# Reciprocal roots of the layernorms: Newton steps on VectorE, or a power on GpSimd

## The chip, the cores and the metric

The kernel runs on one core of a Trainium2 chip. Time is that of one launch on the device, in microseconds (us). The core's engines work side by side, each through a queue of its own in strict order: TensorE (PE in the profile; its weight loads are PEld), VectorE (DVE), ScalarE (ACT), GpSimd (POOL) and SyncE (SP, which issues most transfers). An instruction waits on semaphores until the work of other engines that it needs has ended, and while it waits nothing behind it on the same engine starts.

## The reference

Input x is 2048 rows of 256 float32, with a context of 1601 rows of 256. Four sublayers follow each other; each normalises the rows of x first:

```
x = x + xattn0(layernorm(x), ctx)   # attention, then a second layernorm with gamma and beta
x = x + ffn0(layernorm(x))          # two shared experts and the best two of eight routed ones
x = x + xattn1(layernorm(x), ctx)   # attention in both directions, mixed by a gate
x = x + ffn1(layernorm(x))          # softmax over 8 gates, experts above 0.3, output matrix
layernorm(x) = (x - mean(x)) / sqrt(var(x) + 1e-5)
```

Mean and variance are taken over the 256 values of a row, so each row needs one reciprocal root. The layernorm inside xattn0 works on the same shape.

## The kernel before

Rows lie on 128 partitions, so x is 16 tiles of 128 rows, which stay in the on-chip memory for the whole kernel. A block is four tiles. A layernorm of n tiles runs `bn_stats` and `bn_aggr` for each tile (L179, L180, VectorE), which leaves n means and n variances per partition, and then `rstd_of` (L155) for the n reciprocal roots at once. That is 13 VectorE instructions on 128 x n values: add epsilon (L159), shift the bits right and subtract them from a constant (L161, L162) for a first guess, multiply the variance by -0.5 (L163), and three Newton steps of three instructions (L167, L168, L170). There are 23 such calls: 14 with n = 4, one with n = 8, eight with n = 2.

The order of every engine's queue is made when the program is built: a scheduler places each instruction by its own estimate of durations, so a change of one instruction's engine can move others. The stages, and where the calls lie in them:

- First attention (0 to 150 us and the rest of its last block to 197 us), four blocks of 512 queries. Scores of a block (L268) go to PSUM, ScalarE copies them (L270), VectorE keeps the running maximum (L276). The maxima are transposed (L293, L298, L301), VectorE subtracts them (L308), ScalarE takes the exponent (L311), PE multiplies by the values (L510), ScalarE copies the result (`oT`, L512), and the output projection (L401) reads it. GpSimd adds the 13 score tiles of a block up for the softmax's denominators (L442, L444), a chain of 12 instructions that starts with the next block's first maximum, and adds beta to x (L367). PE reads the sums at L518. The second layernorm (`after`, L393) and the first layernorm of the next sublayer (`settled`, L488, from which L187 makes -mean times root, and ScalarE the scaled rows at L192) are made for one block while the next is under way.
- Shared and routed experts (175 to 578 us). No reciprocal root lies there after 194 us.
- Second attention, first direction (578 to 825 us): the layernorms of four blocks (L948) at 599 to 623 us.
- Second attention, other direction (825 to 1098 us), with the gate and the last sublayer in pairs of tiles that are woven between the attention's matmuls. Here the eight calls with n = 2 lie. For each pair: transposes of the attention's rows (L219, `ob`), gate matmuls (L1105), `z` (L1109, L1110), update of x (L1111, L1113), `bn_stats`, the root, the normalised rows `h` (L201), transposes of `h` (L219), a copy (`hT_g`, L1133), the gates' and experts' matmuls (L1139), a softmax over eight (L1145 to L1159), the sum (L1166) and the store. The attention's value matmuls (L323) fill PE between these steps; the last pair has none left. GpSimd's queue holds indirect transfers there (`near_rows`, L1052) that gather rows of the other direction's result, four for each pair; `sg` (L1063, L1064) mixes them, and its buffers are reused, so later gathers wait for earlier mixes.

Of the kernel before, what the change touches and what calls it, by code (L numbers as in the profile page):

```python
# [9 lines left out]
F32 = mybir.dt.float32  # L10
I32 = mybir.dt.int32
U32 = mybir.dt.uint32
AF = mybir.ActivationFunctionType
ALU = mybir.AluOpType
# [3 lines left out]
P = 128  # L18
# [4 lines left out]
NT = S // P  # L23
# [16 lines left out]
EPS = 1e-5  # L40
# [4 lines left out]
def xattn_ffn_kernel(ctx: ExitStack, tc: tile.TileContext, t: dict, out: bass.AP):  # L45
    nc = tc.nc

    def sbuf(stack, name, bufs=1, side="left"):
        return stack.enter_context(tc.tile_pool(name=name, bufs=bufs, side=side, reuse_waits="tile"))


    const = sbuf(ctx, "const")
# [91 lines left out]

    make_identity(nc, ident)
    nc.gpsimd.memset(ones, 1.0)


    def copy(i, dst, src):
# [4 lines left out]

    def rstd_of(pool, mv, n, wide=BT):  # L155


        ve = pool.tile([P, wide], F32, name="ve")[:, :n]
        nc.vector.tensor_scalar(ve, mv[:, :n, 1], EPS, None, ALU.add)  # L159
        seed = pool.tile([P, wide], I32, name="seed")[:, :n]  # L160
        nc.vector.tensor_scalar(seed, ve.bitcast(I32), 1, None, ALU.logical_shift_right)  # L161
        nc.vector.tensor_scalar(seed, seed, -1.0, float(0x5F3759DF), ALU.mult, ALU.add)  # L162
        nc.vector.tensor_scalar(ve, ve, -0.5, None, ALU.mult)  # L163
        y = seed.bitcast(F32)
        for k in range(3):
            u = pool.tile([P, wide], F32, name="newton")[:, :n]
            nc.vector.tensor_tensor(u, y, y, ALU.mult)  # L167
            nc.vector.tensor_tensor(u, u, ve, ALU.mult)  # L168
            new = pool.tile([P, wide], F32, name=f"rstd{k}")[:, :n]
            nc.vector.scalar_tensor_tensor(new, u, 1.5, y, ALU.add, ALU.mult)  # L170
            y = new
        return y

    def stats_of(first, n, pool, wide=BT):

        st = pool.tile([P, wide, 6], F32, name="st")
        mv = pool.tile([P, wide, 2], F32, name="mv")
        for j in range(n):
            nc.vector.bn_stats(st[:, j, :], xs[:, first + j, :])  # L179
            nc.vector.bn_aggr(mv[:, j, :], st[:, j, :])  # L180
        return mv, rstd_of(pool, mv, n, wide)
# [147 lines left out]
    with ExitStack() as ph:  # L329
# [63 lines left out]
        def after(b, oT, rden, past):  # L393

            st = sp.tile([P, BT, 6], F32, name="st2")
            mv = sp.tile([P, BT, 2], F32, name="mv2")
            for j0 in range(0, BT, 2):
                ps = bank(ps_m)
                for k in range(2):
                    j = j0 + k  # L400
                    nc.tensor.matmul(  # L401
                        ps[:, k * D : (k + 1) * D], oT[:, j * P : (j + 1) * P], wofc, start=True, stop=True
                    )
                for k in range(2):
                    y = past[:, j0 + k, :]
                    nc.vector.scalar_tensor_tensor(
                        y, ps[:, k * D : (k + 1) * D], rden[:, j0 + k : j0 + k + 1], y, ALU.mult, ALU.add
                    )
                    nc.vector.bn_stats(st[:, j0 + k, :], y)
                    nc.vector.bn_aggr(mv[:, j0 + k, :], st[:, j0 + k, :])  # L410
            rs = rstd_of(sp, mv, BT)
            for j in range(BT):
                y, xt = past[:, j, :], xs[:, b * BT + j, :]
                nc.vector.scalar_tensor_tensor(y, y, mv[:, j, 0:1], gamma, ALU.subtract, ALU.mult)
                nc.vector.scalar_tensor_tensor(xt, y, rs[:, j : j + 1], xt, ALU.mult, ALU.add)
# [33 lines left out]
        for b in range(NB + 1):  # L449
            new = between = None  # L450
            if b + 1 < NB:
                h = rows_before(b + 1, fresh(b + 1))
            if b < NB:
# [27 lines left out]
                new = (b, e, acc, past)  # L481
# [19 lines left out]
            else:  # L501
                n, e, acc, past = last
# [357 lines left out]
    with ExitStack() as ph:  # L860
# [117 lines left out]
        for n_blk, blk in enumerate(blocks + [None]):  # L978
            new = between = None
            if blk is not None:  # L980
# [15 lines left out]
                new = (lo, w, e, acc)  # L996
# [18 lines left out]
    with ExitStack() as ph:  # L1015
# [176 lines left out]
        for b in range(NB + 1):  # L1192
            new = between = None
# [3 lines left out]
            if b < NB:  # L1197
# [3 lines left out]
                new = (b, e)  # L1201
# [3 lines left out]
            else:  # L1205
                n, e = last
# [82 lines left out]
```

## Time and profile before

| | us |
|---|---|
| median of three runs (lowest, highest) | 1098.29 (1097.05, 1099.68) |
| profiled execution, own time | 1099.73 |
| its span | 1097.9 |
| PE busy in it | 1052.9 |
| VectorE, ScalarE, GpSimd busy | 504.2, 342.6, 230.3 |

The profiled execution is 1.44 us above the median. Its mean granted TensorE clock is 0.976 of full speed. A line of a timeline gives the start, the duration, engine, line of the program, operation, the tile written and the tiles read, their shapes, and how many instructions were merged; in brackets stands the idle time of that engine just before it, and what ended it.

### The profile page before, as it was taken

To read this page: it belongs to the slowest core of one execution; us is meant where nothing else is said; L and a number is where in the kernel's file an instruction comes from. 1 tells how busy PE (TensorE), PEld (TensorE's weight loads), DVE (VectorE), ACT (ScalarE), POOL (GpSimd) and SP (SyncE) were. 2 spreads that over 40 slices of the span, in tenths; PEclk is the share of its full clock that TensorE was granted. 3 is DMA by queue.
4 is the path that set the end of the run, shared out by engine and by line. 5 is a ranking of instruction groups with operands and counts; after the bars stand their busy time and mean duration, and the time that the engine had idled before them with its cause. 6 is when DMAs were issued, how large, how long until landed. Compare 5 with 4: busy or idle time off the path is not lost. (4 is left out here: it accounts for less than half of the span.)

```text
span 1097.9 us, 11034 instructions
## 1 busy us (share of the span) xinstructions
PE 1052.9 (96%) x3718; PEld 654.4 (60%) x3718; DVE 504.2 (46%) x1271; ACT 342.6 (31%) x569; POOL 230.3 (21%) x236
## 2 busy tenths in 40 slices
PE   7999989999999999999999999999998979999994
PEld 5545548656556666666665644464763466675873
DVE  4777884422222222222223745442413766566764
ACT  3754634311111112112213435321403633333311
POOL 2066440032320011111111006603134312000000
PEclk9999988899999999999999999999999989999997
DMA  9070000911121411111104000010004212000000
GB/s 315 24 188 1 0 1 17 409 73 39 44 54 30 123 44 44 49 44 48 44 24 138 27 0 1 0 39 30 10 19 139 84 38 80 11 10 10 1 20 19
DMA packets 42326, 62.81 MB, mean 57 GB/s; under 512 B 10461, under 2 KB 30045, under 8 KB 42270
## 3 DMA queue, kind: packets, MB, share of 16 engines
q1 hardware_dynamic: 35342, 43.73, 12.4%
q0 software_dynamic: 5824, 17.32, 5.0%
q10 hardware_dynamic: 1104, 1.05, 0.3%
q8 instruction: 31, 0.51, 0.2%
q14 instruction: 25, 0.20, 0.1%
HBM read 42.65 MB, written 19.44 MB: 57 GB/s over the span
## 5 line engine op out<-in xcount | busy, mean ns | idle before, releaser
L794 PE MATMUL sc<-rew,rT 128*128 x288 | 129.6, 593 | 0.6 <-DVE rT L785 0.6
L706 PE MATMUL sc<-hT_f,ew 128*128 128x512 f32 x256 | 115.8, 608 | 0.0
L323 PE MATMUL mm<-vs,e 128*128 128x257 f32 (+1 forms) x416 | 97.8, 386 | 0.0
L268 PE MATMUL sc<-hT,ks 128*128 128x512 f32 (+1 forms) x208 | 91.6, 593 | 3.3 <-DVE m L279 3.3
L308 DVE TENSOR_TENSOR e<-e,tp 128x2048 f32<-128x2048 f32 (+3 forms) x48 | 86.7, 1860 | 12.7 <-PE tp L301 12.7
L311 ACT ACTIVATE e<-e 128x2048 f32<-128x2048 f32 (+3 forms) x48 | 74.3, 1571 | 51.3 <-DVE e L308 50.3
L268 PE MATMUL sc<-qs,hT 128*128 128x512 f32 (+2 forms) x256 | 88.1, 501 | 0.9 <-ACT hT L949 0.9
L1008 PE MATMUL mm<-e,hr 128*128 128x512 f32 (+2 forms) x256 | 88.0, 500 | 0.0
L323 PEld LDWEIGHTS mm<-vs,e 128*128 128x128 f32 (+1 forms) x416 | 79.1, 194 | 13.8 <-issue 2.8
L794 PEld LDWEIGHTS sc<-rew,rT 128*128 128x128 f32 x288 | 54.5, 190 | 54.2 <-issue 52.5
L270 ACT COPY e<-sc 128x512 f32<-128x512 f32 (+3 forms) x116 | 61.0, 534 | 81.7 <-PE sc L268 81.6
L276 DVE TENSOR_TENSOR m<-sc,m 128x512 f32<-128x512 f32 (+3 forms) x100 | 62.7, 627 | 51.8 <-ACT e L270 48.7
L706 PEld LDWEIGHTS sc<-hT_f,ew 128*128 128x128 f32 x256 | 49.6, 196 | 56.9 <-issue 55.8
L800 DVE TENSOR_TENSOR ract<-rsl,sc 128x512 f32<-128x512 f32 x36 | 24.8, 688 | 111.5 <-PE sc L794 108.0
L819 POOL DMA_INDIRECT rows_out<-rout,goes_to x36 | 35.0, 973 | 175.0 <-DVE rout L818 170.6
L268 PEld LDWEIGHTS sc<-qs,hT 128*128 128x128 f32 x256 | 48.0, 190 | 37.1 <-issue 26.8
L1008 PEld LDWEIGHTS mm<-e,hr 128*128 128x128 f32 x256 | 48.2, 190 | 35.3 <-issue 28.2
L268 PEld LDWEIGHTS sc<-hT,ks 128*128 128x128 f32 (+1 forms) x208 | 38.2, 186 | 50.1 <-issue 43.2
L814 PE MATMUL mm<-rew,raT 128*128 x288 | 68.0, 380 | 0.0
L711 ACT ACTIVATE sl<-sc 128x512 f32<-128x512 f32 x32 | 19.1, 597 | 132.4 <-PE sc L706 132.4
L798 ACT ACTIVATE rsl<-sc 128x512 f32<-128x512 f32 x36 | 21.5, 597 | 123.0 <-PE sc L794 123.0
L993 POOL TENSOR_TENSOR acc<-acc,e 128x512 f32<-128x512 f32 (+2 forms) x56 | 57.9, 1033 | 4.4
(267 smaller groups left out, 1459.7 us busy)
## 6 DMA issues: line engine op xcount, KB each, us to landing
rew<-in_ew_dram SPq DMA_DIRECT2D x24, 512.0 KB, 10.2
rows_in<-zero SPq DMA_DIRECT2D x1, 5011.5 KB, 21.5
rin<-rows_in SPq DMA_DIRECT2D x36, 128.0 KB, 2.1
g<-rows_out SPq DMA_DIRECT2D x8, 512.0 KB, 5.6
ew<-in_ew_dram SPq DMA_DIRECT2D x7, 512.0 KB, 5.4
rows_sub<-sgrow SPq DMA_DIRECT2D x12, 256.0 KB, 2.0
ctxT<-in_ctxT_dram SPq DMA_DIRECT2D x4, 512.0 KB, 6.2
out_dram<-xs SPq DMA_DIRECT2D x8, 256.0 KB, 2.1
```

Source lines behind the costliest of these rows:

```text
L268: nc.tensor.matmul(ps, kT[:, d, k * P : k * P + r], q[:, d, :], start=(d == 0), stop=(d == nd - 1))
L270: seen = [nc.scalar.copy(e[:r, k, :w], ps)]
L276: seen.append(nc.vector.tensor_tensor(m[:r, :w], ps, upto, ALU.max))
L308: nc.vector.tensor_tensor(part, part, bc[:r, :w].unsqueeze(1).to_broadcast([r, k1 - k0, w]), ALU.add)
L311: nc.scalar.activation(part, part, AF.Exp)
L323: nc.tensor.matmul(ov[:c, : D + 1], e[:r, k, j * P : j * P + c], v[:r, k, :], start=(k == 0), stop=(k == len(rows) - 1))
L706: nc.tensor.matmul(p, w[:, c, cols], hT[:, c, b * BW : (b + 1) * BW], start=(c == 0), stop=(c == DC - 1),)
L794: nc.tensor.matmul(p, rT[:, c, :], w[:, bass.ds(base + c * HID, HID)], start=(c == 0), stop=(c == DC - 1))
L814: nc.tensor.matmul(y, aT[:, hc, :], routed[2][:, bass.ds(base + hc * D, D)], start=(hc == 0), stop=(hc == NHC - 1))
L819: nc.gpsimd.indirect_dma_start(out=rows_out, out_offset=bass.IndirectOffsetOnAxis(ap=goes_to[:, s : s + 1], axis=0), in_=r, in_offset=None ...
L993: nc.gpsimd.tensor_tensor(acc[:, :w], acc[:, :w], e[:, k, :w], ALU.add)
L1008: nc.tensor.matmul(ov, hr[:, k, d * P : (d + 1) * P], e[:, k, :w], start=(k == 0), stop=(k == NT - 1))
```

## The change

`rstd_of` now takes two GpSimd instructions: the addition of epsilon, and a power, element by element, whose exponents are a tile that holds -0.5 everywhere. That tile is made once. All 13 VectorE instructions of each call go. In the changed file the new lines are L148, L160 and L162.

```diff
     make_identity(nc, ident)
     nc.gpsimd.memset(ones, 1.0)
+    power = const.tile([P, NT], F32, name="power")
+    nc.gpsimd.memset(power, -0.5)
...
         ve = pool.tile([P, wide], F32, name="ve")[:, :n]
-        nc.vector.tensor_scalar(ve, mv[:, :n, 1], EPS, None, ALU.add)
-        seed = pool.tile([P, wide], I32, name="seed")[:, :n]
-        nc.vector.tensor_scalar(seed, ve.bitcast(I32), 1, None, ALU.logical_shift_right)
-        nc.vector.tensor_scalar(seed, seed, -1.0, float(0x5F3759DF), ALU.mult, ALU.add)
-        nc.vector.tensor_scalar(ve, ve, -0.5, None, ALU.mult)
-        y = seed.bitcast(F32)
-        for k in range(3):
-            u = pool.tile([P, wide], F32, name="newton")[:, :n]
-            nc.vector.tensor_tensor(u, y, y, ALU.mult)
-            nc.vector.tensor_tensor(u, u, ve, ALU.mult)
-            new = pool.tile([P, wide], F32, name=f"rstd{k}")[:, :n]
-            nc.vector.scalar_tensor_tensor(new, u, 1.5, y, ALU.add, ALU.mult)
-            y = new
-        return y
+        nc.gpsimd.tensor_scalar(ve, mv[:, :n, 1], EPS, None, ALU.add)
+        rs = pool.tile([P, wide], F32, name="rstd")[:, :n]
+        nc.gpsimd.tensor_tensor(rs, ve, power[:, :n], ALU.pow)
+        return rs
```

## The prediction

> **What bounds the kernel now.** First the page: busy shares, then PE over 40 slices.
>
> ```profile
> PE 1052.9 (96%) x3718; PEld 654.4 (60%) x3718; DVE 504.2 (46%) x1271; ACT 342.6 (31%) x569; POOL 230.3 (21%) x236
> ...
> PE   7999989999999999999999999999998979999994
> ```
>
> PE is full but for the first slice, the last one and a few nines missing between. So a VectorE instruction saved is worth nothing by itself; a reciprocal root counts only where PE stands still for it, and PE's whole idle time is 45 us. Next, the timelines of PE, VectorE and GpSimd around the roots. The last root of all, and PE beside it and before it:
>
> ```profile
> 1081.74 0.17 DVE L159 TENSOR_SCALAR ve<-mv 128x2 f32<-128x2 f32 x1
> ...
> 1084.11 0.73 DVE L201 TENSOR_SCALAR h<-xs,mv,rstd 128x256 f32<-128x256 f32 x2
> ...
> 1066.17 0.78 PE L219 MATMUL tp<-ident,h 128*128 128x128 f32 x4 [0.80 <-DVE h L201]
> ...
> 1074.58 0.55 PE L219 MATMUL tp<-ident,ob 128*128 128x128 f32 x3 [1.28 <-DVE ob L1077]
> ...
> 1084.67 1.13 PE L219 MATMUL tp<-ident,h 128*128 128x128 f32 x4 [6.87 <-DVE h L201]
> ```
>
> A root takes 1084.11 - 1081.74 = 2.37 us, and only the last pair has PE idle for all of it. For the seven pairs before, value matmuls cover the root but for 0.25, 0.45, 0.41, 0, 0.20, 0.82 and 0.80 us (PE's idle time at L219 `h`). Now the first pair, with GpSimd's queue:
>
> ```profile
> 902.81 1.41 POOL L1052 DMA_INDIRECT near_rows<-rows_sub,near  x1 [22.30 <-ACT z L1110]
> ...
> 905.70 0.16 DVE L159 TENSOR_SCALAR ve<-mv 128x2 f32<-128x2 f32 x1
> ...
> 908.07 0.73 DVE L201 TENSOR_SCALAR h<-xs,mv,rstd 128x256 f32<-128x256 f32 x2
> ```
>
> Its root is made while GpSimd issues four gathers, until 908.2. Last, the first attention, where GpSimd's chains of sums lie beside roots:
>
> ```profile
> 93.27 14.77 POOL L444 TENSOR_TENSOR acc<-acc,e 128x512 f32<-128x512 f32 x11
> ...
> 102.03 0.62 DVE L159 TENSOR_SCALAR ve<-mv 128x4 f32<-128x4 f32 x1
> ...
> 105.47 2.29 DVE L308 TENSOR_TENSOR e<-e,tp 128x2048 f32<-128x2048 f32 x1
> ...
> 112.78 3.67 PE L401 MATMUL mm<-wofc,oT 128*128 128x256 f32 x8 [2.71 <-ACT oT L512]
> ...
> 149.44 3.78 PE L401 MATMUL mm<-wofc,oT 128*128 128x256 f32 x8 [3.34 <-ACT oT L512]
> ```
>
> PE waits at L401 for `oT`, which waits on ScalarE for L308's results.
>
> **Price of the new root.** From the variances to the first use: VectorE to GpSimd 0.15 us (an L276 ends at 124.68, L442 starts at 124.83), the addition 0.20, GpSimd's wait on itself 0.07 (sums of 1.27 us follow each other every 1.34), the power p, GpSimd to its reader 0.06 (sums end at 73.66, L518 starts at 73.72): 0.48 + p. No row shows a power. GpSimd's groups that bound it:
>
> ```profile
> L367 POOL TENSOR_TENSOR xs<-xs,beta 128x1024 f32<-128x1024 f32 x4 | 9.4, 2360 | 64.9 <-ACT past L192 49.4 <-DVE newton L167 15.5
> ...
> L993 POOL TENSOR_TENSOR acc<-acc,e 128x256 f32<-128x256 f32 x14 | 10.2, 725 | 1.1
> ...
> L683 POOL COPY h_f<-place_i 128x16 int32<-128x16 int32 x2 | 0.4, 206 | 2.2 <-DMA rows_in<-h_f,slot 2.2
> ...
> L617 POOL CAST e<-e8i 128x8 f32<-128x8 int32 x1 | 0.2, 181 | 0.0
> ```
>
> So p is at least 0.18 (nothing with data is cheaper at this size) and, as its upper end, 2.36, the dearest arithmetic row. With two to eight values per partition it is nearest to the 0.2 us rows; I take 0.40, twice the copy, for the many steps of a power. The root then costs 0.88 us instead of 2.37 (a gain of 1.49) wherever GpSimd is free. Each 0.1 us on p is 0.1 us on every root.
>
> The Trainium skill's GPSIMD Engine Reference (section "Performance versus the Vector engine") speaks against the change: elementwise work stays on VectorE, about 2x faster. The trace agrees for large tiles (1270 ns for 128x512 on GpSimd, 627 ns on VectorE at L276). By that rule two instructions of 0.16 us would be 0.64 instead of my 0.60, so the sum would be 0.4 us higher. The same page (section "Instruction dispatch") puts a first call of a freshly loaded routine at about 6 us; no row here shows that; it would let the first root end at about 14.5 instead of 10.6, and PE wants that block at 17.25, so the sum would stay.
>
> **What else moves.** The order in which the built program queues its work is changed too; these are the places that touch PE.
>
> 1. Cover is taken away. Between the gate matmuls (L1105) and the transposes of `h`, the changed kernel has fewer value matmuls (0.43 us each): 13 for 18 (first pair), 14 for 19 (third), 6 for 11 (fourth), 11 for 16 (sixth and seventh); for the second, six of 12 and two more scores (0.86). That is about 2.15 us, near the scheduler's own gain, and the work is done later. So the 1.49 us are not PE's gain: PE comes 2.15 us earlier and the root 1.49.
> 2. GpSimd's queue has the first root behind the four gathers, and the second behind the next four.
> 3. In the first attention, VectorE's L187 now waits for GpSimd's sums and stands ahead of L308, where Newton steps stood and ran.
>
> **The sum, last stage**, with 0.88 us a root. From `z` to the variances, waits counted from L1105's end, 0.56 from L201's start to PE (as at 908.07 and 908.63), 0.24 for the modelled tail of the cover:
>
> - First pair. `z` started at 900.59; the gathers end 7.6 us later, the root 0.73 after that, PE can transpose at 8.9; its cover ends at 5.6. The wait of 3.2 is partly given back, since ScalarE's copy waits for a gather's landing at 909.6 in either case: L1139 starts at 10.5 for 10.26, with four value matmuls fewer done: +0.24 + 1.72 = +2.0.
> - Second: same queue; transposes at 8.9 for 9.1 but 0.9 us less cover: wait about 1.5 at L219 and L1139 for 0.7: +0.8.
> - Third: `z` to variances 5.45 (two softer steps now come before, L1098 after), 0.2 + 5.45 + 0.88 + 0.56 - 6.26 = 0.8 for 0.41: +0.4. Fourth: 6.95 + 0.88 + 0.56 - 7.98 = 0.4 for 0: +0.4. Fifth: as the third, 0.8 for 0.20: +0.6.
> - Sixth: 0.2 + 3.83 + 0.88 + 0.56 - 4.97 = 0.5 for 0.82: -0.3. Seventh: 0.2 + 3.9 + 0.88 + 0.56 - 4.97 = 0.57 for 0.80: -0.2 (VectorE is free for `z` earlier there, since value matmuls or transposes now precede L1105).
> - Those moved matmuls lie ahead of the last `ob`: 11 for 4, so its 1.28 us wait goes: -1.3. Last pair: no cover, -1.5.
>
> Sum: +0.9.
>
> **The sum, first attention.** The built order starts block 1's sums some 3 us earlier (54.3, their maximum waits no longer for scaled rows), so PE's wait at 73.72 falls by 1.2. In block 2 the sums then end near 104.9, and L187 lets L308 start at 105.8 where it did at 105.47; the lead is lost. In block 3, two L510 are now ahead of the scores, the sums end near 142.5 (before, 140.9), the root at 143.2, and L308 starts 0.9 after 142.43; PE's L401 comes at 150.7 for 149.44: +1.3. No value is given to the roots at 184 to 194: PE has expert matmuls there, and GpSimd is idle. Those at 599 to 623 cost nothing either way: PE reaches the first rows at 617.83, they were ready at 605.6. If that cover were gone, it would be the root's 0.88. The transfers on SyncE keep their order; GpSimd's scatters at 221 start earlier, and PE works on shared experts until past 340.
>
> Together +2.2 us. The profiled execution's 1099.73 would become 1101.9; against the median of 1098.29, 1.44 lower, that is 1100.5. Ten roots lie on PE's path (eight in the last stage, two in the first), so p moves this by 10 us per us: 1098.3 at p = 0.18, 1120 at 2.36.
>
> **The rivals.**
>
> - A dear power. If it takes 1 us or more (2.36: 1120), all gates wait, and VectorE stands still behind L187, L415 and L201. For it: no row of a power, and Newton needs 13 steps. Against: 8 values at most. From p = 0.4 it is slower by over 0.2%. Price at p = 1.2: 1108.5.
> - The other side: PE's holes close. If the moved matmuls fill what PE now waits for, in the pairs 1 to 7 (0.25 + 0.45 + 0.41 + 0.20 + 0.82 + 0.80 = 2.9, and the 1.28), with the last pair's 1.5, the time is 1098.3 - 5.7 = 1092.6. For it: the same amount of value matmuls is left for later places. Against: two roots behind eight gathers. It decides if the root stays within the scheduler's own figure, which the removed cover puts at 2.37 - 2.15 = 0.22 to 0.65, that is p below 0.2, and the gathers start 3 us earlier.
> - No effect: 1098.3, if the queues' losses and the last pair's gain cancel.
>
> **How the numbers follow.** Forecast with p from 0.2 to 0.7 and 3 us for the reordering: 0.50; dear power 0.23; holes closed 0.20; no effect 0.07. A change within 0.2% (2.2 us) is about what a measurement here cannot tell from none. The forecast lies at that bound: slower 0.27, same 0.19, faster 0.04 of its 0.50. Dear power is all slower, closed holes all faster, no effect 0.06 same and 0.01 faster. Together slower 0.50, same 0.25, faster 0.25. The range leaves out the dearer half of the dear powers and the ends of closed holes: 1093.5 to 1115; the forecast's own is 1097 to 1104.
>
> **What would show it.** VectorE 299 instructions fewer (972) and near 450 us busy; GpSimd 47 more. First L162 of n = 2: its start-to-start spacing gives p. GpSimd's first pair: power right behind the fourth gather; PE's idle at that L219 near 3 us; the last L219 idle 5.4 for 6.87; `ob`'s 1.28 gone; PE's L401 waits 4 us twice. Wrong if p is over 1 us, if the gathers start earlier, or if the early stage keeps its lead of 1.2 us.

## The result, and the profile after

The changed kernel takes 1107.62 us (median of six runs, 1104.40 to 1110.78) where the kernel before takes 1098.42 beside it: ratio 1.0086, 95% interval 1.006 to 1.0112. It is slower, by about 9 us. The forecast was 1100.5, its own range 1097 to 1104, its range over all rivals 1093.5 to 1115. The direction and the wide range hold; the likeliest case was 7 us too fast. The profiled execution of the changed kernel took 1110.78 us (span 1108.7, granted clock 0.971), the slowest of the six, 3.2 above the median: differences between the two traces are to be read with that in mind.

First the page: busy times, then PE over 40 slices. All lines after `rstd_of` stand nine lower than before (L201 is now L192, L219 is L210, L401 is L392, L1139 is L1130).

```profile
PE 1056.0 (95%) x3718; PEld 657.0 (59%) x3718; DVE 457.1 (41%) x972; ACT 342.7 (31%) x569; POOL 258.7 (23%) x283
...
PE   8998989999999999999999999999999879999995
```

VectorE has lost 299 instructions and 47.1 us of work. PE stands still for 52.7 us of its span, where it was 45.0, and its 3718 matmuls take 1056.0 us, where they took 1052.9. Next, GpSimd's groups for the new instruction, by shape (count, then busy time and the mean of one in ns):

```profile
L162 POOL TENSOR_TENSOR rstd<-ve,power 128x4 f32<-128x4 f32 x14 | 14.5, 1037 | 1.2
L162 POOL TENSOR_TENSOR rstd<-ve,power 128x2 f32<-128x2 f32 x8 | 5.7, 712 | 0.7
L162 POOL TENSOR_TENSOR rstd<-ve,power 128x8 f32<-128x8 f32 x1 | 1.7, 1655 | 0.1
```

The power p that the forecast put at 0.40 us takes 0.71 for two values per partition, 1.04 for four, 1.66 for eight: 0.39 us and 0.16 more for every value. Next, the last stage: GpSimd around the first gate root, and PE around the first, second, seventh and last (in brackets PE's idle time just before, and what ended it).

```profile
905.62 1.41 POOL L1043 DMA_INDIRECT near_rows<-rows_sub,near  x1 [21.88 <-ACT z L1101]
...
909.95 1.01 POOL L1043 DMA_INDIRECT near_rows<-rows_sub,near  x1 [0.30 <-issue]
910.99 0.25 POOL L160 TENSOR_SCALAR ve<-mv 128x2 f32<-128x2 f32 x1
911.32 0.72 POOL L162 TENSOR_TENSOR rstd<-ve,power 128x2 f32<-128x2 f32 x1
...
912.64 0.45 PE L210 MATMUL tp<-ident,h 128*128 128x128 f32 x1 [3.64 <-DVE h L192]
...
916.10 4.86 PE L1130 MATMUL sc<-ewg,hT_g 128*128 128x264 f32 x16
...
938.08 0.78 PE L210 MATMUL tp<-ident,h 128*128 128x128 f32 x4 [2.32 <-DVE h L192]
...
940.15 4.78 PE L1130 MATMUL sc<-ewg,hT_g 128*128 128x264 f32 x16
...
1075.73 0.78 PE L210 MATMUL tp<-ident,h 128*128 128x128 f32 x4 [0.81 <-DVE h L192]
...
1086.58 0.55 PE L210 MATMUL tp<-ident,ob 128*128 128x128 f32 x3 [0.67 <-DVE ob L1068]
...
1095.45 1.13 PE L210 MATMUL tp<-ident,h 128*128 128x128 f32 x4 [5.60 <-DVE h L192]
```

The root is made right behind the fourth gather, as foreseen, and PE waits 3.64 us for it (foreseen 3.2). The last wait has fallen from 6.87 to 5.60. New are the lines at 916.10 and 940.15: the same 16 matmuls took 3.77 and 3.74 us before. Last, the first attention, GpSimd, VectorE and PE together:

```profile
42.61 1.66 POOL L162 TENSOR_TENSOR rstd<-ve,power 128x8 f32<-128x8 f32 x1
...
51.78 1.12 PE L259 MATMUL sc<-qT,kT 128*128 128x512 f32 x2 [0.96 <-ACT past L381]
...
81.22 0.88 DVE L406 SCALAR_TENSOR_TENSOR xs<-past,rstd,xs 128x256 f32<-128x256 f32 x2 [1.25 <-POOL rstd L162]
...
104.73 0.23 POOL L160 TENSOR_SCALAR ve<-mv 128x4 f32<-128x4 f32 x1
105.04 1.03 POOL L162 TENSOR_TENSOR rstd<-ve,power 128x4 f32<-128x4 f32 x1
106.10 0.16 DVE L178 SCALAR_TENSOR_TENSOR nmean<-mv,rstd 128x4 f32<-128x4 f32 x1 [7.22 <-POOL rstd L162]
...
113.19 3.54 PE L392 MATMUL mm<-wofc,oT 128*128 128x256 f32 x8 [5.89 <-ACT oT L503]
...
151.34 3.78 PE L392 MATMUL mm<-wofc,oT 128*128 128x256 f32 x8 [4.96 <-ACT oT L503]
```

L178 is the L187 of the forecast: it waits for a root that stands behind GpSimd's chain of sums, and VectorE's L299 (once L308) starts behind it. PE's two waits were 2.71 and 3.34.

To place a loss, the traces are compared at three points that every kernel has: PE's first transposes of an expert's rows (366.56 before), the first transposes of the maxima in the last stage (885.10 before), and the last transposes of `h` (1084.67 before). The table gives the first arrival, then the two stretches, all from the timelines of PE in one profiled execution each, and the measured ratio.

| kernel | to the experts | to the last stage | last stage | ratio to before (95% interval) |
|---|---|---|---|---|
| before | 366.56 | 518.54 | 199.57 | 1 |
| changed | 370.96 | 517.17 | 207.32 | 1.0086 (1.006, 1.0112) |
| x1 multiplication, more expert work | 362.02 | | 198.91 | 1.011 (1.009, 1.013) |
| x2 gathers behind two roots | 371.50 | 517.45 | 202.40 | 1.0038 (1.0023, 1.0054) |
| x3 power for the gates only | 367.10 | 521.03 | 204.51 | 1.0054 (1.0035, 1.0073) |
| x4 power for the early roots only | 369.64 | 517.41 | 200.74 | 1.0018 (1.0003, 1.0033) |
| x5 multiplication, same work | 362.88 | 517.36 | 198.92 | 0.9942 (0.9922, 0.9962) |
| x6 power done twice | 377.19 | 517.32 | 212.03 | 1.0208 (1.0174, 1.0243) |
| x7 both places mended | 362.49 | 517.15 | 201.11 | 0.9981 (0.9957, 1.0005) |
| x8 power for the last root only | 367.04 | 521.40 | 199.31 | 0.9984 (0.9964, 1.0005) |
| x9 two early roots by Newton | 368.34 | 517.51 | 203.15 | 1.0017 (0.9997, 1.0038) |
| x10 power where GpSimd is free | 363.12 | 517.36 | 198.31 | 0.9956 (0.9942, 0.997) |
| x11 x10, last wait filled | 364.12 | 517.23 | 200.55 | 0.9939 (0.9919, 0.9958) |
| x12 x10 with two Newton steps | 365.39 | 517.46 | 196.75 | 0.9938 (0.9918, 0.9957) |

In the traces of before and after, the change loses 4.4 us ahead of the experts and 7.75 in the last stage, and gains 1.4 between them. PE's idle time grows by 3.2 us in the first stretch and by 5.65 in the last; the rest, 1.2 and 2.1, is matmuls that take longer.

### The profile page after: what moved, and what is told of

Same layout as the page of the kernel before. It is cut to its first block, busy times and chain, and to the rows that moved or that the text cites. A ratio compares the mean times of both kernels' runs of the same rounds, so it can differ in the third digit from the quotient of the medians.

```text
span 1108.7 us, 10794 instructions
## 1 busy us (share of the span) xinstructions
PE 1056.0 (95%) x3718; PEld 657.0 (59%) x3718; DVE 457.1 (41%) x972; ACT 342.7 (31%) x569; POOL 258.7 (23%) x283
## 3 DMA queue, kind: packets, MB, share of 16 engines
q10 hardware_dynamic: 1104, 1.05, 0.3%
## 4 chain that ended last, share of the span: by engine, by line
PE 79%; DVE 7%; POOL 6%; issue 4%; ACT 3%; DMA 1%; POOLq 0%; DVEq 0%; SPq 0%; ACTq 0%
PE sc L259 13%; PE sc L785 11%; PE sc L697 10%; PE mm L999 8%; PE mm L805 6%; PE mm L712 5%; PE mm L314 5%; PE sc L222 3%; PE sc L1130 3%; POOL acc L435 3%; PE sc L961 2%; DVE e L299 2%; PE mm L501 2%; PE tp L797 1%; POOL near_rows L1043 1%
## 5 line engine op out<-in xcount | busy, mean ns | idle before, releaser
L785 PE MATMUL sc<-rew,rT 128*128 x288 | 129.5, 592 | 0.6 <-DVE rT L776 0.6
L299 DVE TENSOR_TENSOR e<-e,tp 128x2048 f32<-128x2048 f32 (+3 forms) x48 | 86.3, 1860 | 12.5 <-PE tp L292 12.4
L785 PEld LDWEIGHTS sc<-rew,rT 128*128 128x128 f32 x288 | 54.5, 190 | 54.2 <-issue 52.5
L160 POOL TENSOR_SCALAR ve<-mv 128x4 f32<-128x4 f32 (+2 forms) x23 | 6.1, 264 | 243.9 <-DVE mv L171 207.5
```

The lines of the kernel that those rows point to most:

```text
L299: nc.vector.tensor_tensor(part, part, bc[:r, :w].unsqueeze(1).to_broadcast([r, k1 - k0, w]), ALU.add)
L785: nc.tensor.matmul(p, rT[:, c, :], w[:, bass.ds(base + c * HID, HID)], start=(c == 0), stop=(c == DC - 1))
```

## The experiments

**x1 and x5: the power's length taken away.** A multiplication of the same tiles takes the power's place; every instruction stays where it is on its engine. The root is left out in both, so the rows are scaled by something else.

```diff
-        nc.gpsimd.tensor_tensor(rs, ve, power[:, :n], ALU.pow)
+        nc.gpsimd.tensor_tensor(rs, ve, power[:, :n], ALU.mult)
```

> The changed kernel with the power replaced by a multiplication by the same constant tile (so the reciprocal root itself is left out and the rows are scaled by something else); every instruction keeps its place on its engine. A multiplication of 128x2 or 128x4 should take about 0.2 us on GpSimd, against 0.71 and 1.04 for the power. Theory (the dear power is half of the loss, the places of the roots in GpSimd's queue are the other half): eight gates times 0.5 and two early roots times 0.85 are 5.7 us, so 1107.6 - 5.7 = 1102 us, ratio to the kernel before 1.0035; PE's first two long waits at the transposes of h fall from 3.64 and 2.32 to about 3.1 and 1.8 and do not go. Rival 1 (the power's length is all): at or below the kernel before, 1097 to 1098.5. Rival 2 (the order alone, the power's length is covered): 1106 to 1108.

With the constant -0.5 the rows chose other experts, and the expert loop ran 39 times for 36 (its L785 has 312 matmuls for 288). PE was busy 1064.8 us for 1056.0, so its time of 1112.54 us is no comparison. Ahead of the experts and in the last stage its trace can be read, and it agrees with the next run.

x5 has the same edit and one more:

```diff
-    nc.gpsimd.memset(power, -0.5)
+    nc.gpsimd.memset(power, 0.6)
```

> As the first run with a multiplication in the power's place (the reciprocal root is left out, the constant is now 0.6, positive, so that the rows go to the experts in as many blocks as in the kernel before: the first run had 39 trips of the expert loop for 36). Every instruction keeps its place. Theory (price and place both count): as in the first run, PE's wait near 52 us goes (0.96), the two waits at L392 are 4.2 and 4.1 us for 5.9 and 5.0, the waits at the transposes of h 3.1 and 1.75 for 3.64 and 2.32, under 0.5 in the pairs 3 to 7, 5.1 for 5.6 in the last pair: 3.5 + 3.9 = 7.4 us less than the changed kernel, 1100.2, ratio 1.000 to 1.004. Rival 1 (the power's length alone): 1092 to 1097, ratio below 0.998. Rival 2 (the place and order alone): 1105 or more, ratio above 1.006.

Measured: 1094.31 us, ratio 0.9942 (0.9922, 0.9962). That is the number of rival 1, and faster than the kernel before. Groups of GpSimd, then PE's timeline:

```profile
L162 POOL TENSOR_TENSOR rstd<-ve,power 128x4 f32<-128x4 f32 x14 | 2.8, 199 | 1.2
L162 POOL TENSOR_TENSOR rstd<-ve,power 128x2 f32<-128x2 f32 x8 | 1.6, 194 | 0.7
```

```profile
109.26 3.78 PE L392 MATMUL mm<-wofc,oT 128*128 128x256 f32 x8 [4.24 <-ACT oT L503]
147.42 3.78 PE L392 MATMUL mm<-wofc,oT 128*128 128x256 f32 x8 [4.11 <-ACT oT L503]
...
904.45 0.30 PE L210 MATMUL tp<-ident,h 128*128 128x128 f32 x1 [3.11 <-DVE h L192]
...
926.51 0.78 PE L210 MATMUL tp<-ident,h 128*128 128x128 f32 x4 [1.75 <-DVE h L192]
...
1079.16 1.14 PE L210 MATMUL tp<-ident,h 128*128 128x128 f32 x4 [5.08 <-DVE h L192]
```

Every wait is what the theory said, to 0.1 us; the waits of pairs 3 to 7 are below 0.5. But the total is 6 us lower than the theory's, and at the experts PE is already 3.7 us ahead of the kernel before. The long waits behind gathers (3.11, 1.75) and behind sums (4.24, 4.11) are still there, and yet the kernel beats the one before. In sum PE stands still for 44.6 us of the span of 1092.5, as in the kernel before (45.0): shorter waits elsewhere, the last one among them (5.08 for 6.87), make up for the long ones. What is gained is busy time: 3718 matmuls take 1047.9 us for 1052.9.

The changed kernel runs PE's matmuls in the same order as x5 and its loops as often, on other values. So what turns the change into a loss is the power's length, 0.52 us more than the multiplication for two values and 0.84 for four. It is worth 1.0086 less 0.9942, some 16 us. In the two traces half of that is idle time of PE (52.7 for 44.6), and half is matmuls that take longer (1056.0 for 1047.9). That the longer matmuls come from the longer waits is an argument and not shown here; x11 shows it for one wait.

**x6: the power's length doubled.**

```diff
+        rough = pool.tile([P, wide], F32, name="rough")[:, :n]
+        nc.gpsimd.tensor_tensor(rough, ve, power[:, :n], ALU.pow)
         nc.gpsimd.tensor_tensor(rs, ve, power[:, :n], ALU.pow)
```

> The changed kernel with each power done twice, the first into a tile that nobody reads; PE, VectorE, ScalarE and SyncE keep their orders. Theory (each root's length now stands in full on PE's path at eight gates and three early places): 8 times 0.79 and 3 times 1.11 is 9.6 us more than the changed kernel: 1117, ratio 1.015 to 1.020, PE's wait in the pairs 3 to 7 near 1.6 for 0.8. Rival (work beside it covers half): 1112, ratio 1.012.

Measured: 1123.58 us, ratio 1.0208 (1.0174, 1.0243), just above the theory's 1.015 to 1.020. The second power took 0.69 us (two values) and 1.00 (four). PE's timeline:

```profile
118.17 3.78 PE L394 MATMUL mm<-wofc,oT 128*128 128x256 f32 x8 [6.89 <-ACT oT L505]
...
157.99 3.78 PE L394 MATMUL mm<-wofc,oT 128*128 128x256 f32 x8 [5.95 <-ACT oT L505]
...
1086.17 0.78 PE L212 MATMUL tp<-ident,h 128*128 128x128 f32 x4 [1.48 <-DVE h L194]
```

Each wait grew by just the second power: 1.00 at both L394, 0.67 at the seventh pair. Nothing covers it at these places, and waits appear where the changed kernel has little or none (1.87 us at 20.81, for 0.39; 0.80 at 200.55). PE's idle time grows from 52.7 to 64.9 us; its busy time does not grow (1054.9 for 1056.0). Taken with x5, the price can be read by stage: ahead of the experts 362.88, 370.96, 377.19 for the cheap, the single and the double power; the last stage 198.92, 207.32, 212.03; between them nothing (517.2 to 517.4).

**x2: the gathers behind the first two gate roots.** `last_root` collects the powers as the program is built; the lines that fill it are left out here.

```diff
-                    near_rows(i + 6)
+                    with tc.issue_after(last_root[first_gate + i // 2 - 3].ins) if i >= 6 else ExitStack():
+                        near_rows(i + 6)
```

> The changed kernel with the gathers issued during the first two gate roots put behind those roots in GpSimd's queue; PE, VectorE and SyncE keep their order. Theory (queue): the first two roots end about 4 and 1 us earlier, PE's waits of 3.64 and 2.32 us at the transposes of h fall below 1 each, and the 16 matmuls behind them take 3.75 us again for 4.86 and 4.78; minus 4 to 6 us, so 1102 to 1104, ratio 1.004 to 1.005. Rival 1 (the power's length alone): the waits fall by under 0.5 us and the time stays at 1106 to 1108. Rival 2 (the gathers land late instead): a wait of VectorE or ScalarE for near_rows takes the place of the wait for the root and the time stays at 1106 or more.

Measured: 1104.06 us, ratio 1.0038 (1.0023, 1.0054), at the low end of the theory's 1.004 to 1.005. GpSimd, ScalarE and PE around the first gate root:

```profile
908.98 0.23 POOL L162 TENSOR_SCALAR ve<-mv 128x2 f32<-128x2 f32 x1 [24.65 <-DVE mv L174]
909.29 0.72 POOL L164 TENSOR_TENSOR rstd<-ve,power 128x2 f32<-128x2 f32 x1
910.21 1.28 POOL L1046 DMA_INDIRECT near_rows<-rows_sub,near  x1 [0.20 <-issue]
...
916.80 0.72 ACT L1057 ACTIVATE near_rows<-near_rows,rest 128x512 f32<-128x512 f32 x1 [1.97 <-DMA near_rows<-rows_sub,near]
...
910.61 0.30 PE L213 MATMUL tp<-ident,h 128*128 128x128 f32 x1 [0.93 <-DVE h L195]
...
922.24 0.77 PE L213 MATMUL tp<-ident,ob 128*128 128x128 f32 x3 [2.10 <-DVE ob L1071]
```

The root now starts as soon as its variances are there, and the waits of 3.64 and 2.32 become 0.93 and 0.73; the 16 matmuls behind them take 3.74 us. Part of it is handed back, as rival 2 said: the gathers land later, ScalarE waits 1.97 us for one with copies of `hx` behind it, the gates' softmax on VectorE is later, `ob` stands behind that, and PE waits 2.10 for `ob`, where the changed kernel has no wait of half a microsecond.

**x3 and x4: one stage at a time.** A call takes the power or the 13 VectorE instructions by its place (the lines that hand the place `at` on are left out, here and below).

```diff
+        by_power = at[0] == 'gate'      # x3; x4: at[0] != 'gate'
+        return (rstd_power if by_power else rstd_newton)(pool, mv, n, wide)
```

> Power on GpSimd only for the eight gate roots of the last stage, Newton steps on VectorE for all roots before. Theory (losses of two stages add up: about 3 us by 850 us, about 6 us after it): 1098.4 + 6 = 1104.5, ratio 1.0055, with PE's first transposes after 850 us at the times of the kernel before, within 1 us. Rival 1 (the first attention is the place): 1098 to 1100. Rival 2 (the last stage is the only place, the 3 us before it are the clock's): 1107.

> Newton steps for the eight gate roots, power on GpSimd for all roots before. Theory (two stages add up): 1098.4 + 3 = 1101.5, ratio 1.0027, with the loss there by 160 us (L401's equal waits about 5.9 and 5 us for 2.7 and 3.3). Rival 1 (the last stage is the only place): 1098 to 1099. Rival 2 (the early stage is the main place): 1104 to 1107.

Measured: 1.0054 (1.0035, 1.0073) and 1.0018 (1.0003, 1.0033), close to the 1.0055 and 1.0027 of the theory of two stages; their excesses add up to 0.0072 beside the 0.0086 of the whole. x4's interval reaches down to the 1098 to 1099 us of its first rival, so by itself it does not rule that out; its waits for `oT`, 5.90 and 4.96 us, are the expected ones. For x3, PE's arrival at the last stage was not within 1 us of before: 888.13 for 885.10. Its wait for a maximum near 848 us was 3.50 us (2.76 before), and the 12 score matmuls behind it took 8.12, where the kernel before takes 5.63 and a wait of 0.59 between them.

**x9 and x7: the two early roots off GpSimd, alone and with x2's edit.**

```diff
+        by_power = at[0] != 'settled' or at[1] > 1      # the settled rows of blocks 0 and 1 by Newton
```

> The changed kernel with only the two early roots that wait behind GpSimd's chains of sums by Newton steps on VectorE (the gathers stay ahead of the first two gate roots). Theory (x7 was x2 and this, 1.0038 became 0.9981): 5.7 thousandths off the changed kernel's 1.0086, so ratio 1.003 (1.001 to 1.005), of which under 3 us are shorter waits at L401's like and the rest fewer half-clock stretches of PE before 220 us. Rival (this place is worth only the waits, 2.6 us): ratio 1.006 or more.

> Two places mended at once: the gathers behind the first two gate roots, and Newton steps on VectorE for the two early roots that wait behind GpSimd's chains of sums; the other 21 roots stay with the power. Theory: the mended places add up (3.5 us measured for the gathers, about 2.4 for the early roots by the run with Newton gates): 1101.5, ratio 1.001 to 1.004, and PE's waits at L401's like back to 2.7 and 3.3 us. Rival (no adding up, the order of the work alone holds it): 1104, ratio 1.005 or more.

Measured: x9 1.0017 (0.9997, 1.0038), x7 0.9981 (0.9957, 1.0005), the first within its range of 1.001 to 1.005, the second better than its own. PE's two waits for `oT` came to 4.90 and 3.33 us in x7 (5.89 and 4.96 in the changed kernel). The expectation that both would be back at 2.7 and 3.3 failed for the first. x7 and the kernel before cannot be told apart.

x9 gains 0.0069 over the changed kernel, 7.6 us, and its two waits for `oT` (4.90, 3.35) explain 2.6 of them; that is also what its profile is ahead at the experts. Another 4.2 us come in the last stage, which the edit does not touch: there, from the first transposes of the maxima on, x9 has the changed kernel's order on all engines. PE's timeline in x9, at the first two pairs:

```profile
910.58 0.30 PE L233 MATMUL tp<-ident,h 128*128 128x128 f32 x1 [3.62 <-DVE h L215]
...
912.35 3.74 PE L1153 MATMUL sc<-ewg,hT_g 128*128 128x264 f32 x16
...
933.25 0.78 PE L233 MATMUL tp<-ident,h 128*128 128x128 f32 x4 [2.36 <-DVE h L215]
...
934.74 3.74 PE L1153 MATMUL sc<-ewg,hT_g 128*128 128x264 f32 x16
```

The waits for the roots are the same, but the 16 matmuls behind them take 3.74 us for 4.86 and 4.78. Of the 4.2 us, 3.0 are matmul time, and 1.2 a wait for `ob` at the start of the stage (0.78 for 1.97). x7, with x9's order up to the experts, is 8.5 us ahead of the changed kernel there. This difference between two equal orders is the subject of the last section.

**x8: the last root alone.**

```diff
+        by_power = at == ('gate', 14)
```

> Only the very last root by GpSimd's power, all others by Newton steps; PE and ScalarE keep the order of the kernel before and GpSimd's queue is empty there. Theory: this root has no other work beside it; 2.37 us become 0.15 + 0.22 + 0.08 + 0.72 + 0.06 = 1.2, PE's last wait falls from 6.87 to 5.6 to 5.7 us: 1.1 to 1.3 us faster, ratio 0.999 (0.9975 to 1.0005). Rival (GpSimd has been idle and answers late, or its dispatch adds over a microsecond): wait at 6.5 or more, ratio 1.000.

PE's timeline shows the expected wait (it was 6.87):

```profile
1087.75 1.13 PE L233 MATMUL tp<-ident,h 128*128 128x128 f32 x4 [5.64 <-DVE h L215]
```

With GpSimd free, the wait for the root is 1.23 us shorter than with Newton's 2.37. In the total, 0.9984 (0.9964, 1.0005), that cannot be told from nothing.

**x10: the power where it costs nothing.** Power for the first attention's other roots, the second attention's and the last gate; Newton steps for the two roots behind the sums and the first seven gates.

```diff
+        by_power = at == ('gate', 14) or at[0] in ('a0', 'after', 'a1') or (at[0] == 'settled' and at[1] > 1)
```

> Power on GpSimd for all roots before the last stage but the two behind the sums, and for the very last root; Newton steps on VectorE for those two and for the first seven gates. PE's order of the last stage is that of the kernel before. Theory (pieces add up): PE reaches the first expert loop some 4 us earlier than the kernel before, as in x7 (362.5 for 366.6), then 518 to 517, then the last stage with 1.2 us less in the last wait: 1099 - 4 - 1 - 1.2 = 1093, ratio 0.994 (0.991 to 0.998). Rival (x7's early gain was chance of one profile): ratio 0.998 or more.

Measured: 1095.19 us, ratio 0.9956 (0.9942, 0.997). This version beats both kernels. Its profile, the fastest of its twelve runs, has the pieces that the theory named: 3.4 us ahead of the experts, 1.2 between, 1.3 in the last stage. The first piece is not firm: x9 has the same order up to there and is 5.2 us later. The median's gain of 4.8 us leaves some 2.3 for it, as an estimate.

**x11: the last wait filled.** Nine matmuls whose result nobody reads, in PE's last wait.

```diff
...
+                if i == 14:
+                    with tc.issue_after(gm.ins):
+                        spare = bank(ps_s)
+                        for k in range(9):
+                            nc.tensor.matmul(spare, cT[:, 0, 0:P], m[:, 0, :], start=True, stop=True)
```

> x10 with nine matmuls of 128x512, whose result nobody reads, put on PE into its last wait (between the gate matmuls and the transposes of h of the last pair); all orders else the same. Theory (a PE that stands still is given half the clock afterwards, so that a wait costs more than its length): the wait of 5.6 us is filled, L1139's like takes 3.8 to 4.5 us for the 5.5 to 6.7 measured behind every such wait, and the time falls by 1 to 2.5 us against x10, ratio 0.002 lower. Rival (the half clock there comes from something else, or stands by time): L1139's like stays over 5.5 us and the time is x10's or longer by what the nine matmuls overhang (0 to 2 us).

The end of PE's timeline in x10:

```profile
1078.79 1.13 PE L233 MATMUL tp<-ident,h 128*128 128x128 f32 x4 [5.63 <-DVE h L215]
1080.65 5.39 PE L1153 MATMUL sc<-ewg,hT_g 128*128 128x264 f32 x16 [0.73 <-ACT hT_g L1147]
```

and in x11:

```profile
1074.18 7.89 PE L1126 MATMUL sc<-sg,cT 128*128 128x512 f32 x18
1081.90 0.60 PE L233 MATMUL tp<-ident,h 128*128 128x128 f32 x4
1083.23 3.77 PE L1158 MATMUL sc<-ewg,hT_g 128*128 128x264 f32 x16 [0.73 <-ACT hT_g L1152]
```

The 16 matmuls and the four transposes run at full speed once PE has not stood still: 3.77 us for 5.39, 0.60 for 1.13. In all 13 other profiles the 16 matmuls behind the last wait took 5.39 to 6.68 us. The filling (recorded as 18 matmuls, 7.89 us) was too long by 1.9 us and took back what it gave: 0.9939 (0.9919, 0.9958) is not told from x10.

**x12: two Newton steps for three in x10**, which leaves out the refinement of the last digits.

```diff
-        for k in range(3):
+        for k in range(2):
```

> x10 with two Newton steps for three in the roots that stay on VectorE (the third step, a refinement of the last digits, is left out): 3 instructions of 0.17 us less in each of nine roots, and the order of the work is planned anew. Theory (a gate root's length stands on PE's path at the seven gates): 7 times 0.5 at most, since covers there are 0.2 to 0.8 us short: 2 us less than x10, ratio 0.992. Rival (the order planned anew takes cover away, as with the power): x10's time or up to 4 us more.

Measured: 1094.28 us, 0.9938 (0.9918, 0.9957). The trace has 1.6 us less in the last stage than x10; the total is not told from it.

## Why the prediction was right or wrong

- **Price of the new root: the step that failed.** "I take 0.40, twice the copy": measured 0.71 for the gates, 1.04 and 1.66 for the rest, within the bounds of 0.18 and 2.36. The reason given, that two to eight values are nearest to the 0.2 us rows, is refuted by x5 and the changed kernel together: a multiplication costs 0.194, 0.199, 0.202 us for two, four and eight values, a power 0.16 for each value. The nearest size is no guide to an operation that works long on each value. The sign "p is over 1 us" was met by the roots of four and eight values, not by the gates. (The 627 ns given for VectorE's L276 is a mean over several shapes; 128x512 takes 692, so the ratio to GpSimd's 1270 is 1.8.) The 0.48 around it was right: the last root's wait is 1.27 shorter, so the root takes 2.37 - 1.27 = 1.10 against 0.48 + 0.71 = 1.19.
- **The sum of the last stage: right where the matmuls keep their speed.** With the measured 0.71 in the place of 0.40, the foreseen waits of pairs 1 to 7 are 3.5, 1.8, 1.1, 0.7, 1.1, 0.8, 0.9 and the last 5.7; the trace has 3.64, 2.32, 0.85, 0.71, 0.79, 0.76, 0.81 and 5.60. Only `ob`'s 1.28 did not go, it fell to 0.67. The sum becomes 0.9 + 8 x 0.31 = +3.4. x9, in the same order, has 203.15 for 199.57, +3.6. At x5's 0.19 the steps give 0.9 - 8 x 0.21 = -0.8, and x5 has -0.65. The changed kernel's own profile has +7.75: a longer wait for the first `ob` and slower matmuls, neither of which the forecast had.
- **The first attention: right in kind, two roots short.** Waits of "4 us twice" are what x5 shows (4.24, 4.11), and PE's L392 came at 113.19 and 151.34 for the foreseen "no lead" and 150.7. But "ten roots lie on PE's path, two in the first" left out two more: the root of eight values at 42.6, after which PE waits 0.96 at 51.78, and the second layernorm's at 80.1, for which L406 waits 1.25 (0.40 in x5). Between x5 and the changed kernel PE falls back by a further 2.2 - 0.9 = 1.3 by 56 us (0.9 was there at 19 us already) and by 1.7 more by the first L392: half of that is L406's root, half the one behind the sums, which was counted. x6 adds the first block's root (the wait at 20.81).
- **The cover of the roots at 184 to 194 and 599 to 623: right, and a gain was missed.** No wait appears there (with the doubled power, 0.80 us at 200.55). The stretch from the experts to the last stage takes 517.2 to 517.5 us in all ten kernels with the same expert work that make the second attention's roots on GpSimd (x5 with the multiplication), for 518.5 before and 521.0 and 521.4 in the two others that keep Newton there. The difference lies in PE's wait for a maximum near 848: 1.3 to 1.8 us, against 2.76, 3.50 and 3.81, the last two with slow matmuls behind them. Why that order is kinder was not tried.
- **"p moves this by 10 us per us": right for the gates, too low for the whole.** From the multiplication to the power, 0.52 us more on eight gates and 0.84 on two early roots make 5.8 by that rule; measured 16. From one power to two, 7.5 by the rule and 13.4 measured. For the eight gates the rule holds: x5 to x9, in one order of the last stage, 4.2 us for 8 x 0.52 = 4.2. The early roots that were left out raise the waits: PE's idle time grows by 8.1 us in the first step and by 12.2 in the second. The 8.1 us of longer matmuls in the first step are a term that the forecast put at nothing; in the second step they do not grow.
- **The clock.** The forecast counted each wait at its length. In the changed kernel the 16 matmuls after the waits of 3.64 and 2.32 us took 4.86 and 4.78 us for 3.77 and 3.74, and x11 shows for the last wait that standing still is the cause. The Trainium skill's TensorE: Matmul & The Clock Gate (section "What's actually happening") says that PE falls to half its clock after about 3.4 us without work, as seen by a window that runs freely, and that the same code therefore falls differently from run to run. The trace agrees for the last wait (5.08 to 6.87 us, slow each time) and for waits near 3.5 us, which are slow in some profiles: the 16 matmuls behind 3.64 in the changed kernel, the scores behind 3.50 in x3, only the first few matmuls behind x3's 3.70 (its 16 took 3.67), none behind 3.62 in x9. Behind the 2.32 us the matmuls were slow in the changed kernel alone (3.74 behind 2.39 in x3 and 2.36 in x9); that wait is shorter than the page's window, and what slowed them is open.
- **The rivals.** The dear power was the right one, at a lower threshold than "1 us or more": its formula at p = 1.2 gave 1108.5, the time came at p = 0.71 to 1.04 to 1107.6. All gates wait, and VectorE stands still behind L178, L406 and L192, as it said. "PE's holes close" gave 1092.6 and decided "below 0.2"; x5 has p = 0.19 and 1094.3. But that agreement is luck: in x5 the holes did not close (the first two waits are 3.11 and 1.75 for 0.25 and 0.45), and the gain is busy time. That the chances went by a guessed p was the weakness.
- **The total.** 1100.5 with the p measured (8 x 0.31 + 2 x 0.64 = 3.8) is 1104.3. The medians leave 3.3 us. In the two traces PE's idle time grew by 7.7 us where the sum with this p has 6.0, and its matmuls by 3.1 us where it has nothing; the two together are 1.5 us more than the medians leave, for the profiled execution lies 3.2 us above the median with the changed kernel and 1.3 with the kernel before. So the unforeseen part is early roots left out, a longer wait for the first `ob` and longer matmuls; how it divides in the median is not shown.

## What to carry to other kernels

Here an arithmetic instruction's price on another engine was not bounded usefully by its size. Where no row shows the operation itself, the forecast should be split by its price before anything else, because here the sign of the whole change hung on 0.2 or 0.7 us. Moving an operation to a seldom used engine paid where that engine's queue was empty and the reader waited for nothing else (the last root: a wait 1.23 us shorter), and lost behind gathers and chains of sums, so it should be moved call by call. A wait of over 5 us on PE is to be priced above its length: the 16 matmuls behind it took 1.6 to 2.9 us more in 13 profiles. Behind waits of 2.3 to 3.7 us that happened in some profiles only.

## What the runs showed of the hardware that was not expected

GpSimd's power costs 0.39 us and 0.16 us for each value of a partition, and its first call in the program (1.03 us at 8.26, 0.1 us behind the end of the addition) costs no more than the later ones of its shape (1.037). The last is against the 6 us of a first call that the forecast weighed from the Trainium skill's GPSIMD Engine Reference (section "Instruction dispatch"): no run here shows it.

One and the same order of work reaches the experts at times that differ by 5.9 us, more than the 4.4 that the change costs up to there in its traces. x7, x9, x10 and x11 have one order on PE and VectorE until after 890 us; their profiles have PE at the experts at 362.49, 368.34, 363.12 and 364.12. The windows of PE from 150 to 220 us (start and end, length, PE's busy time, granted clock, DMA share, GB/s) show where, in x9:

```profile
150.00:220.00 70.00, 70.00 (x283) 0.80 0.44 175
```

and in x10:

```profile
150.00:220.00 70.00, 70.00 (x291) 0.86 0.46 182
```

PE is busy throughout in both, at 0.80 of its clock in the one and 0.86 in the other, 0.06 of 70 us or 4.2 us of work. The changed kernel has 0.78 there, the kernel before 0.83, x5 0.87. What sets the clock in this stretch, which follows the two long waits and holds many small matmuls, was not settled: it moved with the waits, and also without them.

The mean granted clock of every run is on record, and within one kernel the time goes with it. The kernel before, in its 76 runs beside x1 to x12, took 1103.66 to 1104.65 us in the seven runs at 0.968, and 1094.97 to 1100.19 in the ten at 0.976. x10 took 1093.64 to 1095.91 in the eleven at 0.979 and 1100.46 in the one at 0.974. The medians of these two groups of the kernel before, 1103.99 and 1097.51, are apart by more than half of what the change costs, so a difference of a few microseconds needs several runs of both kernels.
